# Regrouping an attention loop on TensorE: score and value matmuls in longer runs, four tiles of exponentials, and two smaller buffers paid for it

## The chip, the cores and the metric

The kernel runs on one core of one Trainium2 chip. The metric is the device time of one launch in microseconds (us). The kernel before takes 4168.1 us, the median of three runs that lie between 4166.77 and 4168.17 us. The profiled execution spans 4169.3 us.

## The reference

One vision-transformer layer on 16 images. For each image:

```
h    = patches(x) @ W.T + b                    # 1024 tokens of 768 numbers -> 256
q, k, v = split(layernorm(h) @ w_qkv)          # 8 heads of 32
k    = sum_f a_f*sin(f*k) + b_f*cos(f*k)       # f = 1..256, elementwise ("kan")
h   += softmax(q @ k.T / sqrt(32)) @ v @ w_out + b_out
y    = layernorm(h)
h   += shared_mlp(y) + sum over the top 2 of 4 experts of weight * expert(y)
```

All of it is float32. The Fourier transform of the keys is done by angle addition: a slow wave (two tiles `w`, sines of multiples of 16) is mixed on TensorE with coefficients into `kan`, multiplied on VectorE by a fast wave (`f`), and summed over rows by a matmul with a 0/1 matrix (`red`).

## The kernel before

**Tiling of the work.** An image has 32 groups of keys (`NG`), worked on in rounds of 4 (`GS`): 8 rounds an image, 128 rounds in all. A pair of heads and half of the queries make one attention step (`att`), and each round also does one attention step, two rounds behind the keys it needs. An attention step has eight tiles of keys (`kc` 0 to 7). For each there is a `score` (matmul into PSUM tile `sT`, L1085, followed by `exponential` on ScalarE into an SBUF tile `es`, L1100) and a `weigh` (matmuls of `es` with the values into the PSUM tile `av`, L1117). The value matmul's weights hold 32 columns of values and 32 of ones, so row sums come along.

**Order of TensorE.** Everything is emitted by a planner written in Python (`run`, L398) that holds a modelled clock for each engine and a queue of steps for each. TensorE's own queue is fixed: in a round, the wave mixing (`mix`, L978) and first half of the sums (`add_up`, L1007), then the attention step. The fixed order of the attention step comes from the loop in L1234: with s for a score, r for the second half of the sums, w for a weigh, it is `ssss r ww ss ww ss wwww`. Everything else of the layer (tokens, norms, keys, queries, values, projections, gates and networks) lies in four chains of pieces that the planner inserts between fixed steps, when the next fixed step would have to wait by its model, or when a chain has work due (`PACES`, L57: for each chain a pace per us of fixed work and a limit of what can fall due).

**Matmuls in tiles.** Three kinds of fixed step use a part of the array at a time, so that several matmuls run side by side (`TILINGS`, L59): `kan` in 64x32, `av` in 128x64, `red` in 128x32. Scores and almost all pieces of the chains use the whole array. The planner charges 0.18 us in its model (`SWITCH`) for going from one form to another.

**Buffers the change touches.** `es` tiles come from a ring of three (`esp`, L92); an exponential therefore waits for the weigh of three tiles before (L1103). PSUM has two large tiles (`big`), shared by scores and `kan`, so a score waits for the exponential two scores back. Chunks of x (128 tokens, 384 KB) come from a ring of `XBUFS` = 3 (L45); after a chunk is used the load of the chunk three later is queued (L495). In `keys` (L513) VectorE divides keys by a turn: the integer number of turns goes to tile `n` (L536, a buffer of its own), and after the reduction the angle goes to two tiles `u` and `ui` of a ring of two each (`rup`, tags "u" and "r"), which DMAs write to DRAM (L552). `split` (L558) uses the same two tags for the high and low parts of queries and keys, which DMAs also carry off.

Of the kernel before, what the change touches and what calls it, by code (L numbers as in the profile page):

```python
# [18 lines left out]
P = 128  # L19
# [4 lines left out]
NT = N // P  # L24
# [16 lines left out]
INT = mybir.dt.int32  # L41
FPR = mybir.dt.float32r
BAND0 = 88
XT = 128
XBUFS = 3  # L45
SUM_MAX = 1e20
PACK0 = 18
NW = 8
# [5 lines left out]


LAG, LANDS, TABLE, PER_COLUMN, SWITCH, IDLE = 0.06, 2.0, 1.28, 1.0 / 600, 0.18, 0.3
PACES = ((0.155, 2), (0.44, 2), (0, 0), (0.178, 2.6))  # L57

TILINGS = {"mix": (64, 32), "av": (128, 64), "red": (128, 32)}  # L59

@with_exitstack
def plain_path(ctx: ExitStack, tc: tile.TileContext, a: dict, out: bass.AP, verdict: bass.AP):
# [14 lines left out]
    def pool(name, bufs, space=None):  # L77
        kw = {} if space is None else {"space": space}
        return ctx.enter_context(tc.tile_pool(name=name, bufs=bufs, **kw))

    const = pool("const", 1)
    xp = pool("xp", XBUFS)
    hp = pool("hp", 6)
# [3 lines left out]
    kup = pool("kup", 1)  # L87
    rup = pool("rup", 2)
    wp = pool("wp", NW)
    fp = pool("fp", GS)  # L90
    srcp = pool("srcp", 1)
    esp = pool("esp", 3)  # L92
    q4p = pool("q4p", 2)
    ffp = pool("ffp", 1)
    ff2 = pool("ff2", 2)
# [140 lines left out]
    def retile(tiling):  # L236

        same = now["tiling"] == tiling
        now["tiling"] = tiling
        return 0.0 if same else SWITCH  # L240

    def together(at, queue):

        (cost, _, key, _), *rest = queues[PE][queue][:2]
        tiling = TILINGS.get(key[0])
        if tiling is None or now["tiling"] == tiling or not rest or rest[0][2][0] != key[0]:
            return at
        then = begin(PE, rest[0][1])
        return at + 2 * IDLE if then is None else max(at, then - cost)
# [6 lines left out]
    def side_tile(name):  # L256

        i = chains[now["chain"]]["bank"] = banks(now["chain"])[0][1]
        return side.tile([P, 512], FP, tag=f"side{i}", name=name)
# [91 lines left out]
    def lay(engine, queue):  # L351
        cost, deps, key, action = queues[engine][queue].pop(0)
        at = begin(engine, deps)
        if engine == PE:
            cost += retile(TILINGS.get(key[0]))
        clock[engine] = at + cost
        done[key] = clock[engine]
        if engine == PE:
            for ch, (pace, most) in zip(chains, PACES):
                ch["due"] = min(ch["due"] + pace * cost, most)  # L360
# [37 lines left out]
    def run():  # L398

        while True:  # L400
            soonest = others(clock[PE])
            fixed = min(heads(PE), default=None)
            then = fixed and together(fixed[0], fixed[2])
            follows = fixed and TILINGS.get(queues[PE][fixed[2]][0][2][0]) == now["tiling"] != None
            pieces = [
# [69 lines left out]
    def tokens(b, half):  # L475
# [5 lines left out]
        for t in range(4):  # L481
# [12 lines left out]
            del chunks[b, j]  # L494
            load_x(b, j + XBUFS)  # L495
            yield DVE, 0.41
# [16 lines left out]
    def keys(b, rows, blks=(0, 1)):  # L513

        st = images[b]
        if b >= 2:
            yield "load", NG * (b - 1) - 1, 1
            yield "source", (NG * (b - 1)) // 8 - 1
        if "ud" not in st:
            st["ud"] = udp.tile([E, 2, 2, N], INT, tag="ud", name="ud")  # L520
        for blk in blks:
            yield "hnT", b, blk
            yield GO
            ps = side_tile("k")
            for c in range(2):
                matmul(
                    out=ps,
                    lhsT=wk[:, c, ts(rows, P)],
                    rhs=hnT[:, c, ts(blk, 512)],
                    start=(c == 0),  # L530
                    stop=(c == 1),
                )
            held = chains[now["chain"]]["bank"]
            yield DVE, 1.4
            chains[now["chain"]]["bank"] = held
            n = kup.tile([P, 512], INT, tag="n", name="turns")  # L536
            nc.vector.tensor_scalar(n, ps, INV_2PI, None, ALU.mult)
            nc.vector.scalar_tensor_tensor(ps, n, -TWO_PI_A, ps, ALU.mult, ALU.add)
            yield DVE, 1.4
            chains[now["chain"]]["bank"] = held  # L540
            for part in (TWO_PI_B, TWO_PI_C):
                nc.vector.scalar_tensor_tensor(ps, n, -part, ps, ALU.mult, ALU.add)
            yield DVE, 1.4
            u = rup.tile([P, 512], FP, tag="u", name="u")
            ui = rup.tile([P, 512], INT, tag="r", name="ui")
            uh = u.bitcast(INT)
            nc.vector.tensor_scalar(u, ps, INV_2PI_REST * 2.0**31, None, ALU.mult)
            nc.vector.scalar_tensor_tensor(ui, ps, INV_2PI * 2.0**31, u, ALU.mult, ALU.add)
            yield POOL, 1.02
            nc.gpsimd.tensor_tensor(uh, ui, quarter.to_broadcast([P, 512]), ALU.add)  # L550
            for i, x in enumerate((uh, ui)):
                nc.sync.dma_start(  # L552
                    out=st["ud"][ts(rows, P), i, :, ts(blk, 512)],
                    in_=x.unsqueeze(1).to_broadcast([P, 2, 512]),
                )
            done["rows", b, rows, blk] = sent(2.7, 1.2)
# [156 lines left out]
    def gates(b, half, late=False):  # L713
# [20 lines left out]
        now["stream"] += 2 * P  # L734
        now["piece"] = TILINGS["red"]
        yield ACT, 0.25
# [17 lines left out]
    def networks(b, half, late=False):  # L754
# [29 lines left out]
        def second_of_experts(u, e1):  # L784
            yield GO
            ps = side_tile("e2p")
            now["piece"] = TILINGS["av"]
            now["stream"] -= 512
# [291 lines left out]
    def score(att, kc):  # L1080
        def action():
            q4 = bands_of_queries[att]
            ps = scores[kc] = big.tile([P, 1024], FP, tag="big", name="sT")
            for s in range(2):
                nc.tensor.matmul(  # L1085
                    out=ps[:, ts(s, 512)],
                    lhsT=k4[:, 2 * s + kc // 4, ts(kc % 4, P)],
                    rhs=q4[:, s, :],
                    start=True,
                    stop=True,  # L1090
                )

        deps = [("stacked", att // 2), ("q4", att)] + big_deps(("exp", att, kc))
        put(PE, "fixed", 0.47, deps, ("score", att, kc), action)

    def exponential(att, kc):
        def action():
            now["table"] = AF.Exp
            es = exps[kc] = esp.tile([P, 1024], FP, tag="es", name="es")
            nc.scalar.activation(es, scores.pop(kc), AF.Exp, scale=SCALE)  # L1100

        deps = [("score", att, kc)]
        old = att * NT + kc - 3  # L1103
        if old >= 0:
            deps.append(("av", *divmod(old, NT)))
        put(ACT, "fixed", 0.99, deps, ("exp", att, kc), action)

    def weigh(att, kc):

        p = att // 2  # L1110

        def action():
            if kc == 0:
                acc[0] = avp.tile([P, 512], FP, tag="av", name="av")
            es = exps.pop(kc)
            for s in range(2):
                nc.tensor.matmul(  # L1117
                    out=acc[0][ts(s, 64), :],
                    lhsT=v[:, kc, p % NPAIR, ds(HD * s, 64)],
                    rhs=es[:, ts(s, 512)],  # L1120
                    start=(kc == 0),
                    stop=(kc == NT - 1),
                )

        deps = [("exp", att, kc)]
        if kc == 0:
            b, i = divmod(p, NPAIR)
            deps.append(("all values" if i == NPAIR - 1 else "values", b))
            if att > 0:
                deps.append(("norm", att - 1))  # L1130
        put(PE, "fixed", 0.86, deps, ("av", att, kc), action)
# [49 lines left out]
    queues[SP]["source"] = []  # L1181
    for j in range(XBUFS):
        load_x(0, j)
# [32 lines left out]
    for rd in range(B * RI + 2):  # L1216
        groups = range(GS * rd, min(GS * rd + GS, total))
        att = rd - 2
        attends = 0 <= att < ATT
        for g in groups[::2]:  # L1220
            first = g == groups[0]
            for i, j in ((0, 0), (0, 1), (1, 0), (1, 1), (0, 2), (1, 2)):
                sine(g + i, j, TABLE if first and i == j == 0 else 0.0)
            mix(g)
            mix(g + 1)
        if groups:
            add_up(groups[0] // 2)

        def table():
            now["table"] = AF.Exp  # L1230
            nc.scalar.activation(spare[:, 1:2], spare[:, 0:1], AF.Exp)  # L1231

        put(ACT, "fixed", TABLE + 0.2, [], ("table", rd), table)
        for n in range(0, NT + 2, 2):  # L1234
            if attends and n < NT:
                for kc in (n, n + 1):
                    score(att, kc)
                    exponential(att, kc)
            if n == 2 and groups:
                add_up(groups[0] // 2 + 1)  # L1240
            if attends and n > 0:
                for kc in (n - 2, n - 1):
                    weigh(att, kc)
    with tc.manual_schedule():
        run()

# [746 lines left out]
```

## Time and profile before

| what | value |
|---|---|
| median time | 4168.1 us |
| TensorE busy | 4027.4 us, 97% of the span |
| ScalarE, GpSimd, VectorE busy | 3286.3, 3195.8, 2830.2 us |
| DMA engines busy | 79% on the main queue, 219 GB/s |
| `av` matmuls | 965.1 us busy |
| `sT` matmuls | 691.7 us busy |
| `kan` matmuls | 623.9 us busy |
| exponentials | 1024 of 1022 ns |

Busy time counts each engine's own work; the matmuls' ends are modelled, so a busy TensorE may still be emptying its array or loading weights. The chain of waits is read backwards from the last instruction and names, for every stretch, the engine that held the program up there.

### The profile page before, as it was taken

To read this page: it belongs to the slowest core of one execution; us is meant where nothing else is said; L and a number is where in the kernel's file an instruction comes from. 1 tells how busy PE (TensorE), PEld (TensorE's weight loads), DVE (VectorE), ACT (ScalarE), POOL (GpSimd) and SP (SyncE) were. 2 spreads that over 40 slices of the span, in tenths; PEclk is the share of its full clock that TensorE was granted. 3 is DMA by queue.
4 is the path that set the end of the run, shared out by engine and by line. 5 is a ranking of instruction groups with operands and counts; after the bars stand their busy time and mean duration, and the time that the engine had idled before them with its cause. 6 is when DMAs were issued, how large, how long until landed. Compare 5 with 4: busy or idle time off the path is not lost.

```text
span 4169.3 us, 67564 instructions
## 1 busy us (share of the span) xinstructions
PE 4027.4 (97%) x22753; PEld 1766.4 (42%) x22753; DVE 2830.2 (68%) x4172; ACT 3286.3 (79%) x3939; POOL 3195.8 (77%) x2323
## 2 busy tenths in 40 slices
PE   6889999999999999999999999999999999999998
PEld 4324344443434445344444444444444444443334
DVE  4667767677676776767767677776767767677652
ACT  2688888788787888878788888788788788888873
POOL 3988877778787887878787787888778787787850
PEclk9999999999999999999999999999999999999999
DMA  7988878888787887978878878887887978878740
GB/s 223 263 241 222 243 200 223 238 218 247 207 232 219 239 235 210 244 211 224 247 209 238 221 225 225 228 241 209 234 228 219 251 211 239 219 211 226 197 138 16
DMA packets 587478, 914.27 MB, mean 219 GB/s; under 512 B 58828, under 2 KB 177524, under 8 KB 587124
## 3 DMA queue, kind: packets, MB, share of 16 engines
q1 hardware_dynamic: 580880, 906.98, 78.7%
q8 instruction: 184, 3.01, 0.3%
q10 hardware_dynamic: 6244, 2.88, 0.3%
q14 instruction: 170, 1.39, 0.1%
HBM read 758.64 MB, written 150.99 MB: 218 GB/s over the span
## 4 chain that ended last, share of the span: by engine, by line
PE 74%; ACT 10%; DVE 6%; DMA 5%; issue 3%; SPq 2%; POOL 1%; ACTq 0%; DVEq 0%; POOLq 0%
PE av L1117 18%; PE sT L1085 11%; PE kan L987 9%; PE tok L263 6%; PE e3p L263 5%; PE red L1020 5%; PE e1p L263 5%; ACT w L963 4%; DMA w<-ud 3%; PE s1p L263 3%; PE q L263 2%; PE v L263 2%; PE proj L263 2%; DVE f L1001 2%; PE k L263 2%
## 5 line engine op out<-in xcount | busy, mean ns | idle before, releaser
L953 POOL TENSOR_TENSOR w<-w,lane 128x1024 int32<-128x1024 int32 x1024 | 1926.1, 1896 | 444.4 <-DMA w<-ud 298.6
L1100 ACT ACTIVATE es<-sT 128x1024 f32<-128x1024 f32 x1024 | 1033.0, 1022 | 550.0 <-PE av L1117 339.8
L953 POOL TENSOR_TENSOR f<-f,lane 128x1024 int32<-128x1024 int32 x512 | 971.0, 1896 | 251.2 <-DVE f L938 157.5
L963 ACT ACTIVATE w<-w 128x1024 f32<-128x1024 int32 x1024 | 1021.1, 1048 | 42.1 <-POOL w L953 39.1
L1117 PE MATMUL av<-es,v 128*64 128x512 f32 x4096 | 965.1, 602 | 1.0 <-DVE rc L1162 1.0
L1143 DVE RECIPROCAL rc<-av 128x256 f32<-128x256 f32 x256 | 434.0, 1730 | 702.6 <-PE av L1117 702.6
L1085 PE MATMUL sT<-q,k 128*128 128x512 f32 x2048 | 691.7, 449 | 42.0 <-DVE f L1001 20.2
L1001 DVE TENSOR_TENSOR f<-kan,f 128x1024 f32<-128x1024 f32 x512 | 608.5, 1218 | 159.8 <-ACT f L963 123.7
L938 DVE STREAM_SHUFFLE f<-src 128x1024 int32<-128x1024 int32 x512 | 673.0, 1353 | 0.7
L987 PE MATMUL kan<-w,coef 64*32 64x512 f32 x8192 | 623.9, 600 | 39.5 <-ACT w L963 35.6
L1085 PEld LDWEIGHTS sT<-q,k 128*128 128x128 f32 x2048 | 346.0, 189 | 440.5 <-issue 219.0
L963 ACT ACTIVATE f<-f 128x1024 f32<-128x1024 int32 x512 | 516.1, 1048 | 2.6 <-POOL f L953 2.6
L1117 PEld LDWEIGHTS av<-es,v 128*64 128x64 f32 x4096 | 258.5, 136 | 563.2 <-issue 498.2
L263 PE MATMUL tok<-wt,x 128*128 128x256 f32 x1536 | 362.3, 387 | 16.9 <-DMA w1s<-in_sW 13.6
L263 PEld LDWEIGHTS tok<-wt,x 128*128 128x128 f32 x1536 | 288.7, 192 | 110.8 <-issue 34.7
L987 PEld LDWEIGHTS kan<-w,coef 64*32 64x32 f32 x8192 | 127.9, 105 | 375.2 <-ACT w L963 222.5
L1020 PE MATMUL red<-f,pack 128*32 128x512 f32 x2048 | 273.6, 604 | 1.5 <-DVE f L1001 1.3
L263 PE MATMUL e1p<-hT,w1e 128*128 128x512 f32 x480 | 233.2, 608 | 0.4 <-ACT e L799 0.4
L462 ACT ACTIVATE hn<-h,less,rstd 128x256 f32<-128x256 f32 x256 | 143.8, 591 | 51.6 <-POOL less L454 51.2
L963 ACT ACT_TABLE_LOAD x128 | 164.2, 1283 | 22.4 <-DMA w<-ud 20.2
L1150 DVE TENSOR_TENSOR aT<-av,rc 32x512 f32<-32x512 f32 x256 | 176.1, 688 | 6.4
L1231 ACT ACT_TABLE_LOAD x128 | 164.2, 1283 | 2.2
(125 smaller groups left out, 3746.7 us busy)
## 6 DMA issues: line engine op xcount, KB each, us to landing
w<-ud SPq DMA_DIRECT2D x2048, 256.0 KB
q<-qd SPq DMA_DIRECT2D x512, 128.0 KB
k<-kd SPq DMA_DIRECT2D x128, 512.0 KB
x<-in_xT SPq DMA_DIRECT2D x128, 384.0 KB
ud<-u SPq DMA_DIRECT2D x64, 512.0 KB
ud<-ui SPq DMA_DIRECT2D x64, 512.0 KB
src<-ud SPq DMA_DIRECT2D x512, 64.0 KB
qd<-qhi SPq DMA_DIRECT2D x64, 256.0 KB
```

The costliest lines, as they stand in the source:

```text
L263: nc.tensor.matmul(out=out, lhsT=lhsT, rhs=rhs, start=start, stop=stop)
L938: nc.vector.stream_shuffle(w, sources[g // 8].rearrange("p r n -> p (r n)"), [4 * (g % 8) + i // 8 for i in range(32)],)
L953: nc.gpsimd.tensor_tensor(w, w, f.to_broadcast([P, N]), ALU.mult)
L963: nc.scalar.activation(x, w, AF.Sin, scale=TURN * 2.0**-32)
L987: nc.tensor.matmul(out=ps[ds(64 * j + 32 * blk, 32), ts(r, 512)], lhsT=coef[ts(r, 64)].rearrange("p e f j -> p (e f j)"), rhs=w[ts(r, 64), ...
L1001: nc.vector.tensor_mul(w, kan.pop(g), w)
L1020: nc.tensor.matmul(out=rows_of_pair[p][ts(2 * i + r, 32), :], lhsT=pack[:, ds(PACK0 - 16 * (k % 2) - 2 * (k // 2), 32)], rhs=prod[:, ts(r, ...
L1085: nc.tensor.matmul(out=ps[:, ts(s, 512)], lhsT=k4[:, 2 * s + kc // 4, ts(kc % 4, P)], rhs=q4[:, s, :], start=True, stop=True,)
L1100: nc.scalar.activation(es, scores.pop(kc), AF.Exp, scale=SCALE)
L1117: nc.tensor.matmul(out=acc[0][ts(s, 64), :], lhsT=v[:, kc, p % NPAIR, ds(HD * s, 64)], rhs=es[:, ts(s, 512)], start=(kc == 0), stop=(kc == ...
L1143: nc.vector.reciprocal(rc[0][:, part], acc[0][:, part])
L1150: nc.vector.tensor_mul(aT[ds(64 * (i % 2) + HD * s, HD), i // 2, ts(qb, 512)], acc[0][ds(96 * s, HD), :], rc[0][ds(HD + HD * s, HD), :],)
```

## The change

The attention step's order is written as a string, and its two runs of weighs are made longer: `ssss r ss www ss wwwww`. That needs one more tile of exponentials, since six scores stand ahead of the first weigh. A tile of exponentials is 4 KB a partition; the memory comes from a chunk of x (3 KB) and the tile of whole turns (2 KB), which now takes its place in the ring tagged "u". The chains' paces are set anew.

```diff
-XBUFS = 3
+XBUFS = 2
...
-PACES = ((0.155, 2), (0.44, 2), (0, 0), (0.178, 2.6))
+PACES = ((0.18, 1.5), (0.42, 2.5), (0, 0), (0.16, 2))
...
+ES = 4
+ATTENTION = "ssssrsswwwsswwwww"
...
-    esp = pool("esp", 3)
+    esp = pool("esp", ES)
...
-            n = kup.tile([P, 512], INT, tag="n", name="turns")
+            n = rup.tile([P, 512], INT, tag="u", name="turns")
...
-        old = att * NT + kc - 3
+        old = att * NT + kc - ES
...
-        for n in range(0, NT + 2, 2):
-            if attends and n < NT:
-                for kc in (n, n + 1):
-                    score(att, kc)
-                    exponential(att, kc)
-            if n == 2 and groups:
+        scored, weighed = iter(range(NT)), iter(range(NT))
+        for kind in ATTENTION:
+            if kind == "r" and groups:
                 add_up(groups[0] // 2 + 1)
-            if attends and n > 0:
-                for kc in (n - 2, n - 1):
-                    weigh(att, kc)
+            elif kind == "s" and attends:
+                kc = next(scored)
+                score(att, kc)
+                exponential(att, kc)
+            elif kind == "w" and attends:
+                weigh(att, next(weighed))
```

## The prediction

> **What bounds the kernel now.** I read the shares of busy time first, then the busy time of one image's stretch from the middle, then TensorE's waits, and last the chain of waits inside one attention step.
>
> ```profile
> PE 4027.4 (97%) x22753; PEld 1766.4 (42%) x22753; DVE 2830.2 (68%) x4172; ACT 3286.3 (79%) x3939; POOL 3195.8 (77%) x2323
> ```
> ```profile
> 2000.00:2260.00 260.00, 257.07 (x1477) 117.53 (x1478) 184.72 (x273) 211.16 (x253) 201.08 (x146) 1.00 0.80 224
> ```
> The second line (us, then busy time of PE, PEld, DVE, ACT, POOL, then clock, DMA share and GB/s) says that in the middle TensorE is busy 257 of 260 us, at full clock, and that no other engine passes 211. So TensorE's stream of instructions is the bound, and only what shortens it, or removes a wait in it, counts.
>
> ```profile
> PE kan L987 <- ACT w L963: 35.6, 41, 3.7
> PE sT L1085 <- DVE f L1001: 20.2, 46, 1.0
> PE sT L1085 <- ACT es L1100: 15.4, 38, 1.0
> PE tok L263 <- DMA w1s<-in_sW: 13.6, 1, 13.6
> ```
> These are the longest of TensorE's waits (us in total, times, longest). They are small, so waits alone can't bring much. But TensorE is not doing useful columns all of its busy time. The chain of waits in one attention step (start, us, what):
>
> ```profile
> 2010.06 0.93 PE sT L1085 x4
> ...
> 2013.64 0.99 PE red L1020 x8
> 2014.64 1.87 PE av L1117 x8
> 2016.50 1.12 PE sT L1085 x4
> 2017.63 1.87 PE av L1117 x8
> 2019.49 1.13 PE sT L1085 x4
> 2020.62 3.58 PE av L1117 x16
> ...
> 2028.71 1.88 PE kan L987 x32
> ...
> 2033.46 1.36 PE kan L987 x16
> ...
> 2037.42 1.02 PE kan L987 x16
> ```
> Eight more av matmuls in one run cost 3.58 - 1.87 = 1.71 us, so a run of eight carries 1.87 - 1.71 = 0.16 us that don't depend on its length. Four sT matmuls cost 0.93 us between other whole-array matmuls and 1.12 to 1.13 between runs of av: 0.20 us for standing between two runs of another form. For kan, 1.88 - 1.02 = 0.86 for sixteen, so 1.02 - 0.86 = 0.16 a run. These fixed parts are counted as busy.
>
> **What the Trainium skill says.** "TensorEngine Tiling (Array Packing)", Tiling Modes, Key Properties: changing the tiling mode, as against the tile, drains TensorE. It gives no price; this trace agrees, with 0.16 to 0.20 us a run. "TensorE: Matmul & The Clock Gate", Part 1, on the architecture: ScalarE's and VectorE's queues are strict FIFO, so a VectorE instruction that waits holds all behind it. The trace agrees as far as it shows: the cast to qhi waited 6.8 us for the DMA that carries ui off, and VectorE did nothing meanwhile.
>
> **The change part by part.**
>
> *Fewer changes of form (gain).* Before, a step's fixed order has three runs of av (ww, ww, wwww), afterwards two (www, wwwww); whole-array runs stay three, and the sums one. That is one run less in 128 steps, unless pieces of the chains cut runs. I counted the runs of equal form in the order in which both built programs give TensorE its matmuls: 1863 before and 1707 after. Of 128x64 (av and the experts' second layer) 433 to 311, of the whole array 762 to 746, of kan's form 349 to 332, of red's 286 to 285. All other matmuls are the same in number. So 122 x 0.16 + 16 x 0.20 + 17 x 0.16 = 19.5 + 3.2 + 2.7 = 25.4 us less, all on the path, since it comes out of TensorE's own stream.
>
> *Waits of scores on exponentials.* Each score reuses the PSUM tile of two scores before. Let the step start at 0: scores take 0.46, an exponential 1.03. Exponentials end at about 1.55, 2.6, 3.6 and 4.65. Score 3 can start at 2.6, both before and after; then red to 4.05, the return to the whole array 0.2, score 4 to 4.7, and score 5 needs the end of the fourth exponential at 4.65: it needs no wait. After www (2.6 + 0.16), scores 6 and 7 need exponentials 4 and 5, which start when the first and second weigh free their tiles and take 1.03 each; the second ends about with the start of score 7. So 0; where no piece fills in, 0.3 us in some 40 steps, 12 us, is the upper bound.
>
> *ScalarE free sooner (gain).* With three tiles the last exponential waits for weigh 4; three weighs of 0.86 are left on TensorE, so ScalarE turns to the next sines 3 x 0.86 - 1.03 = 1.55 us before TensorE's end of the step. With four tiles it waits for weigh 3 and is free 4 x 0.86 - 1.03 = 2.4 us before: 0.86 us sooner. This is worth something only where kan waits for a sine: 35.6 us in 41 waits, 0.87 in the mean. Bounds 0 and 35; I take 10, since sines also queue behind other ScalarE work that moves with the paces.
>
> *Two chunks of x.* The load of chunk j+2 now starts when chunk j is used. From the end of a chunk's matmuls to landing, the trace has about 3 us at the start (the packets of 512 bytes are x's alone) and 3 to 8 us later. In the order after, the tightest places in the middle leave 7 us of TensorE work, so I take no wait there. At the start, tokens stand back to back, 2.6 us a chunk, and landing takes 3.1 to 3.8: about 0.5 us every second chunk and 0.8 at the first. For the eight chunks of image 0: 2 us, straight into the span; bounds 1 and 4.
>
> *Whole turns in the ring of angles.* n, u and the low parts now alternate between two buffers. A u follows the u before by one n, so it waits until that one's DMA has landed. A u is reusable after 0.68 (u) + 0.69 (ui) + 1.04 (GpSimd's quarter turn) + 4.4 (from issue to landing, where qhi waited for ui's) = about 7 us. In the order after, VectorE has only 4.1 to 4.9 us of work between two u at seven places: three at the start and four in the middle. In four more places n follows a klo by 2.1 us, and klo's DMA must land: 0.69 + about 4.4 - 2.1 = 3 us. At the start about 3 us each; the first waves need only the first two u, which stand 12 us apart, so I charge 3 (bounds 0 and 7). In the middle 8 x 3 = 24 us of VectorE waiting; what is queued behind are shuffles and products f, and through the products (which free kan's PSUM) TensorE. VectorE is idle 75 of 260 us, so most is absorbed: 6 (bounds 0 and 24).
>
> *Paces.* They move pieces only; what they do to the runs is in the count. 0.
>
> Sum: -25.4 + 0 - 10 + 2 + 3 + 6 = -24.4 us: 4168.1 - 24.4 = 4143.7, say 4144.
>
> **The rivals.** (A) *More than the runs:* ScalarE's head start removes kan's waits (35.6 us) instead of a third of them, and the new waits are absorbed: -25 - 35 + 5 = -55, 4113. For it: the head start equals the mean wait. Against: the longest wait is 3.7 us, so the sum has few long ones that 0.86 doesn't remove. (B) *A new wait takes the gain:* VectorE's wait for the angles' DMAs reaches TensorE in full (24 + 7), x costs 4, kan gains 10: -25 + 31 + 4 - 10 = 0; with half of it, 4160. For it: VectorE is strict FIFO, and DMA is busy 80%, so landing can be slow. Against: the idle share. (C) *Slower:* B in full (0), and steps without a piece wait on exponentials (12), and DMAs land in 8 us, the slowest of x's landings, instead of 4.4: 3.6 us more at 15 places, 54 us, of which I let a quarter reach TensorE (13): 4168 + 25 = 4193. For it: in the first 320 us DMA is the busiest part, where VectorE already waited 6.8 us. Against: sizes and number of the DMAs are as before.
>
> **How the numbers follow.** Forecast 0.63, A 0.14, B 0.15, C 0.08. The range is 4116 to 4166: below, two thirds of A's way; above, most of B; C is left out. Faster by over 0.2% (below 4159.8) are the forecast, A and a part of B: 0.82; within 0.2% 0.10; slower 0.08.
>
> **What would show it.** Right: runs of av of 12 and 20 matmuls in the chain, each 0.16 over 1.71 for eight; TensorE's busy time down by about 25 us; kan's wait for ScalarE below 30; a wait of u or turns on the DMA of ud or kd of some 3 us at some ten places on VectorE, and a few tok waiting for x in the first 40 us. Wrong: if TensorE's idle time grows by more than 20 us, with f or the ring at the head of its waits, or if ScalarE's waits for av don't shrink from 339.8 us.

## The result and the profile after

The changed kernel takes 4194.47 us (median of four runs, 4192.8 to 4204.7) against 4168.04 us: ratio 1.0069, with a 95% interval of 1.0052 to 1.0087. It is slower by 26 us, where 4144 us had been forecast. The profiled executions span 4169.3 and 4190.8 us, 21.5 us apart; the accounts below are of these.

The line of busy times of the changed kernel:

```profile
PE 4008.7 (96%) x22753; PEld 1777.1 (42%) x22753; DVE 2832.2 (68%) x4172; ACT 3273.8 (78%) x3939; POOL 3194.1 (76%) x2323
```

TensorE is busy 4027.4 - 4008.7 = 18.7 us less. But its idle time went from 4169.3 - 4027.4 = 141.9 to 4190.8 - 4008.7 = 182.1 us, 40 us more. The busy time of the same stretch in the middle (us, then PE, PEld, DVE, ACT, POOL, clock, DMA share, GB/s):

```profile
2000.00:2260.00 260.00, 254.78 (x1487) 112.55 (x1485) 185.16 (x268) 214.25 (x257) 207.16 (x149) 1.00 0.83 227
```

TensorE is still the bound, at full clock. Its idle time in the stretch has grown from 2.9 to 5.2 us. The changed kernel's waits of TensorE (us in total, times, longest):

```profile
PE kan L989 <- ACT w L965: 42.3, 43, 4.8
PE sT L1087 <- ACT es L1102: 33.6, 62, 4.0
PE sT L1087 <- DVE f L1003: 17.0, 43, 1.2
...
PE tok L265 <- DMA x<-in_xT: 5.9, 5, 1.8
PE v L265 <- DVE qlo L567: 4.6, 5, 1.2
```

Scores now wait 33.6 us for exponentials (15.4 before), `kan` waits 42.3 us for sines (35.6 before; the forecast had it shrink), and tokens wait for x. Pieces of the chains wait longer too: by the groups of the profile, TensorE's idle time went from 0.4 to 7.3 us ahead of `e1p`, from 0.8 to 6.2 ahead of `gate` and from 0.5 to 5.5 ahead of `v`, and fell from 6.4 to 2.5 ahead of `wb`. One step of attention, from the chain of waits of the changed kernel (start, us, what):

```profile
2014.36 1.91 ACT es L1102 x2
2016.27 0.04 issue
2016.32 0.74 PE sT L1087 x2
2017.05 0.99 PE red L1022 x8
2018.05 1.92 PE k L265 x4
2019.96 0.94 PE sT L1087 x4
2020.90 2.73 PE av L1119 x12
2023.62 1.12 PE sT L1087 x4
```

The chain comes to this step through ScalarE: score 3, the first line of TensorE, starts only when the second of two exponentials has ended. The run of twelve `av` matmuls takes 2.73 us, just what the forecast's price gives (0.16 + 12 x 1.71 / 8 = 2.73). A piece (`k`) now stands between the sums and the fifth score, a place where the kernel before needed none, since two weighs stood there.

**Where the 21.5 us are.** I cut TensorE's stream of each trace into its runs of equal form. From the start of one run to the start of the next there are three parts: the columns of its matmuls at the interval that they keep inside long runs, the fixed price of one run (0.16 for `kan`, 0.15 for 128x64, 0.10 for `red`, 0.20 for the whole array), and a rest, which is mostly waiting. From the first matmul to the last:

```
us                               before   after
columns                          3530.9  3530.9
fixed price of the runs           302.1   277.5   (-24.6; forecast -25.4)
rest: waiting                     314.2   360.2   (+46.0; forecast about +1)
```

The second line is the count of runs times the price of one; that the price holds is shown by the long runs, which take what it gives. The third is what is left, and it grows by about as much as TensorE's idle time in the profile (40 us). To place it, I took for each score the time since the start of the matmul ahead of it, less the time that the quickest tenth of such pairs of matmuls takes in these traces. Ahead of the eight scores of a step this sums to 62 us before and 90 us after; scores 1, 3 and 5 grow by 8 to 9 us each (the fifth from 0.3 to 9.5), the others by less than 2. Another 8.5 us are new in the first eight rounds, where x is loaded (some 2 of them ahead of scores), and about 11 us are spread over the rest of the stream. So the gain of the runs came as forecast, and new waits took it and more.

### The profile page after: what moved, and what is told of

It is laid out like the page before. It is cut to its first block, busy times and chain, and to the rows that moved or that the text cites. A ratio compares the mean times of both kernels' runs of the same rounds, so it can differ in the third digit from the quotient of the medians.

```text
span 4190.8 us, 67571 instructions
## 1 busy us (share of the span) xinstructions
PE 4008.7 (96%) x22753; PEld 1777.1 (42%) x22753; DVE 2832.2 (68%) x4172; ACT 3273.8 (78%) x3939; POOL 3194.1 (76%) x2323
## 4 chain that ended last, share of the span: by engine, by line
PE 62%; ACT 14%; DMA 11%; DVE 6%; issue 3%; SPq 2%; POOL 1%; ACTq 0%; DVEq 0%; POOLq 0%
PE av L1119 15%; PE sT L1087 10%; PE kan L989 7%; ACT w L965 6%; DMA w<-ud 5%; PE tok L265 5%; PE e3p L265 5%; PE e1p L265 4%; PE red L1022 4%; ACT f L965 3%; PE proj L265 2%; PE s1p L265 2%; DVE f L1003 2%; PE k L265 2%; PE v L265 2%
## 5 line engine op out<-in xcount | busy, mean ns | idle before, releaser
L1102 ACT ACTIVATE es<-sT 128x1024 f32<-128x1024 f32 x1024 | 1015.6, 1022 | 540.6 <-PE av L1119 294.0
L1119 PE MATMUL av<-es,v 128*64 128x512 f32 x4096 | 935.4, 598 | 0.1
L1087 PE MATMUL sT<-q,k 128*128 128x512 f32 x2048 | 707.6, 452 | 57.9 <-ACT es L1102 33.6
L989 PE MATMUL kan<-w,coef 64*32 64x512 f32 x8192 | 606.6, 601 | 44.9 <-ACT w L965 42.3
L1087 PEld LDWEIGHTS sT<-q,k 128*128 128x128 f32 x2048 | 337.2, 189 | 512.1 <-ACT es L1102 251.4
L1119 PEld LDWEIGHTS av<-es,v 128*64 128x64 f32 x4096 | 271.3, 136 | 532.7 <-issue 508.8
L552 POOL TENSOR_TENSOR u<-ui,quarter 128x512 int32<-128x512 int32 x64 | 66.4, 1038 | 132.4 <-DVE ui L550 127.5
```

What stands on the lines that cost most here:

```text
L989: nc.tensor.matmul(out=ps[ds(64 * j + 32 * blk, 32), ts(r, 512)], lhsT=coef[ts(r, 64)].rearrange("p e f j -> p (e f j)"), rhs=w[ts(r, 64), ...
L1087: nc.tensor.matmul(out=ps[:, ts(s, 512)], lhsT=k4[:, 2 * s + kc // 4, ts(kc % 4, P)], rhs=q4[:, s, :], start=True, stop=True,)
L1119: nc.tensor.matmul(out=acc[0][ts(s, 64), :], lhsT=v[:, kc, p % NPAIR, ds(HD * s, 64)], rhs=es[:, ts(s, 512)], start=(kc == 0), stop=(kc == ...
```

## The experiments

All ratios are to the kernel before on the same chip, with 95% intervals. For room, kernels with four tiles of exponentials and three chunks of x use the keys' weights for the queries and the values' weights for the output projection (same shapes, other numbers).

**The parts of the change, one at a time.** First the two buffers, each alone:

```diff
-XBUFS = 3
+XBUFS = 2
```

> The kernel before with only two chunks of x in place of three; TensorE's order is unchanged. Theory W, its smaller part: 2 to 8 us at the start, where the tokens stand back to back: 4170 to 4176. Theories O and P: within 6 us of 4168.

Measured: 4179.33 us, 1.0027 [1.0016, 1.0039], or +11 us by the ratio (8 between the medians of that chip). The run's waits of TensorE have a new line, `tok` on the load of x:

```profile
PE tok L263 <- DMA w1s<-in_sW: 13.4, 1, 13.4
PE lnT L267 <- ACT hn L462: 8.4, 9, 3.5
PE tok L263 <- DMA x<-in_xT: 6.5, 5, 1.8
```

From the first matmul to the end of the eighth round this kernel takes 309.9 us instead of 299.4. Later it loses nothing; its profiled execution even gets 6 us back, which the median doesn't show. So the place was right and the size was not: 8 to 11 us, not 2.

```diff
-            n = kup.tile([P, 512], INT, tag="n", name="turns")
+            n = rup.tile([P, 512], INT, tag="u", name="turns")
```

> The kernel before with only the whole turns put into the ring of angles; TensorE's order is unchanged. Theory W: VectorE waits for the DMAs of angles, and TensorE with it, +15 to +35 us: 4183 to 4203. Theories O and P: within 6 us of 4168.

Measured: 4170.09 us, 0.9999 [0.9992, 1.0006]. The turns in the ring cost nothing. In the changed kernel too, VectorE waits less than 1 us in all for a DMA ahead of `u` or the turns, where the forecast had 24 us in the middle alone.

The new paces alone, and the new order alone with the old paces (three chunks of x, a tile of its own for the turns):

```diff
-PACES = ((0.155, 2), (0.44, 2), (0, 0), (0.178, 2.6))
+PACES = ((0.18, 1.5), (0.42, 2.5), (0, 0), (0.16, 2))
```

> The kernel before with only the new paces. 1793 runs of equal form on TensorE against 1863, priced at about 12 us. Theory F (the order with six scores in front opens waits that the pieces of the chains must fill, and the paces only move pieces): within 15 us of before, 4156 to 4172. Theory P (these paces suit the kernel in themselves): 4150 or below, as the new order lost 40 us without them.

```diff
+ES = 4
+ATTENTION = "ssssrsswwwsswwwww"
-    esp = pool("esp", 3)
+    esp = pool("esp", ES)
```

> The kernel before with only the new order of the attention step and four tiles of exponentials (paces, three chunks of x and the own tile of turns as before). To make room, queries are computed with the keys' weights and the output projection with the values' weights: same work, other numbers. TensorE's runs of equal form: 1664 against 1863 before, priced at 0.15 to 0.20 us each about 32 us. Theory W (the two smaller buffers brought the new waits): this kernel keeps the gain, about 4168 - 32 = 4136, with no more idle time of TensorE than before. Theory O (the new order itself makes TensorE wait for exponentials): idle time of TensorE grows by 25 us or more and the time is 4160 or over.

Measured: paces alone 4187.32 us, 1.0038 [1.0024, 1.0053], or +16; order alone 4228.59 us, 1.0148 [1.0131, 1.0165], or +62, with only 1664 runs of equal form and 401 us of waiting. The expectation for the paces alone, within 15 us and not above 4172, failed. Their waits show that a new placing of the pieces makes scores wait for exponentials in the old order too (15.4 us before):

```profile
PE sT L1085 <- ACT es L1100: 28.0, 33, 3.5
```

Both together:

> The kernel after, its order on TensorE instruction for instruction, but with three chunks of x and the own tile of turns; queries and output projection with other weights to make room, as in the run with the order alone. 1707 runs of equal form. Theory W: the new waits go with the buffers, about 4194 - 46 = 4148. Theory P (the paces put pieces where they wait): still near 4190, while the run with the order alone is 25 us or more faster. Theory O: both near 4190.

Measured: 4187.98 us, 1.0052 [1.0036, 1.0069], or +22; fixed prices 277.5 us, waiting 352.9 us, and 30 us more ahead of scores than before, as in the changed kernel (28). So the buffers aren't the cause of the main loss: with the old ones it is there. The paces don't add up with the order: +16 alone, -40 on top of it. A price of their own can't be given.

**The ring of the angles' tiles.** The planner knows nothing of when the DMAs let go of these tiles, and VectorE waited for them in the changed kernel (VectorE's waits):

```profile
DVE khi L566 <- DMA ud<-ui: 19.9, 5, 7.1
DVE qhi L566 <- DMA qd<-qhi: 13.7, 7, 2.9
DVE qhi L566 <- DMA ud<-ui: 10.5, 2, 7.3
```

That is 44 us, where the same three have 16.8 us before. To see what of it reaches TensorE, the ring was made three deep (for room, w1s and w3e are aliased as well):

```diff
-    rup = pool("rup", 2)
+    rup = pool("rup", 3)
```

> The new order with four tiles and new paces (three chunks of x, own tile of turns), and the ring of angles and of high and low parts three deep in place of two. To make room, queries, output projection, the first shared layer and the experts' last layer are computed with other weights. TensorE's order is unchanged. Theory R (part of the new waits is TensorE behind VectorE, which waits until an angles' or a part's DMA has landed): the waits of q and v, about 11 us above before's, go: 10 to 15 us under the run with two tiles. Theory S (waits before scores are all of it): within 5 us of it.

Measured: 4173.7 us, 1.0002 [0.9993, 1.0011], 14 us (medians) to 21 us (ratios) below the same kernel with two; waiting falls by 10 us, to 343.1. So a part of the loss goes through this ring, by the split into high and low parts and not by the turns. But the waits ahead of scores stay (28 us above before), and the gain of the runs still doesn't come out. Then the old order with four tiles and the new paces, with two and three tiles in the ring:

```diff
-ATTENTION = "ssssrsswwwsswwwww"
+ATTENTION = "ssssrwwsswwsswwww"
```

> The old order of the attention step (ssss r ww ss ww ss wwww) with four tiles of exponentials and the new paces; three chunks of x, own tile of turns; queries and output projection computed with other weights to make room. 1815 runs of equal form, priced at about 9 us under before. Theory F (the order makes the waits): 4150 to 4168, and TensorE's unpriced waits no more than before's. If the fourth tile or the new paces make them: 4180 or more, as with the new order.

> The old order with four tiles and the new paces, which took 4296 us, with the ring of angles and parts three deep (the first shared layer and the experts' last layer also with other weights to make room). TensorE's order is unchanged. Theory R: the 79 us by which q and v wait longer than before's go for the most part: 4210 to 4240. If the order of pieces itself makes them: 4280 or more.

Measured: 4295.92 us, 1.0298 [1.0281, 1.0316], and 4241.64 us, 1.0158 [1.0141, 1.0175]. In the first, TensorE's waits show how a late DMA reaches it, through VectorE's queue:

```profile
PE q L265 <- DVE qlo L567: 42.6, 8, 7.2
PE sT L1087 <- ACT es L1102: 32.7, 56, 4.5
PE kan L989 <- ACT w L965: 30.8, 43, 3.7
PE v L265 <- DVE qlo L567: 15.2, 7, 4.3
```

VectorE's waits in the same kernel:

```profile
DVE qhi L566 <- DMA ud<-ui: 42.6, 6, 8.5
DVE qhi L566 <- DMA qd<-qhi: 40.8, 7, 7.3
```

A projection `q` waits for its PSUM bank, which `qlo` must empty, and `qlo` stands behind a `qhi` that waits for a DMA. In the old order, with the pieces placed anew around a fourth tile, the kernel is 124 us slower than before and some 108 slower than with the new paces alone; 54 of these go through the ring. What the tile does with all else in place was not measured in the old order. Scores wait 32.7 us for exponentials here, as long as in the changed kernel: the new order is not the only thing that makes such waits.

**Which engine makes the scores wait?** Half of each exponential is left out (both heads' values are weighed with those of the first), with the old order and with the new one:

```diff
-            nc.scalar.activation(es, scores.pop(kc), AF.Exp, scale=SCALE)
+            nc.scalar.activation(es[:, 0:512], scores.pop(kc)[:, 0:512], AF.Exp, scale=SCALE)
```

> The kernel before with each exponential over half of its columns only (the first head's; its exponentials are also weighed with the second head's values), which takes about 0.4 us off each of 1024. TensorE's order is unchanged. It is the partner of the next run. All theories: somewhat faster, 4130 to 4165.

> The new order with four tiles and new paces (three chunks of x, own tile of turns, queries and output projection with other weights), with the same halved exponentials. Compared with the halved exponentials in the old order. Theory S (in the six scores in front TensorE waits for exponentials): those waits go, and the fewer runs show: 15 to 25 us faster than the partner. Theory F in the wide sense (pieces are short in other places too, at the first two scores and in kan): still slower or within 8 us of the partner.

Measured: 4132.83 us, 0.9908 [0.9891, 0.9924], and 4133.18 us, 0.9909 [0.9893, 0.9926]. Both gain, and the new order's loss of 22 us shrinks to nothing; ahead of score 5, 0.3 us are left. But the expected lead of 15 to 25 us over the old order doesn't appear either: the fixed prices are 24.6 us lower, and the waits still 24 us higher than in the old order (299 against 275 us). Halving the exponentials takes away the loss, not all that stands against the gain. Now the sines instead: of one sine in each pair only half the columns are computed, and used twice.

```diff
-            nc.scalar.activation(x, w, AF.Sin, scale=TURN * 2.0**-32)
+            half = slice(0, 512 if j == 1 else N)
+            nc.scalar.activation(x[:, half], w[:, half], AF.Sin, scale=TURN * 2.0**-32)
```

> The kernel before with every second sine of the slow waves over half of its columns (those columns are mixed twice, the other half is left out), which takes 0.43 us off each of 512 sines, 1.7 us of ScalarE a round between the attention steps. TensorE's order is unchanged. It is the partner of the next run. Theory A (ScalarE, full between the steps, sets the pace there): 4110 or below. Theory T (TensorE alone does): 4150 or more.

> The new order with four tiles and new paces (three chunks of x, own tile of turns, queries and output projection with other weights), with the same shortened sines. Theory A: with ScalarE relieved the 24.6 us of fewer changes of form stay, so 12 to 30 us faster than its partner with the old order. If pieces and waits on DMAs alone eat the gain: no faster than its partner, or slower by up to 17 us as with whole sines.

Measured: 4133.28 us, 0.9912 [0.9895, 0.9928], and 4149.45 us, 0.9951 [0.9934, 0.9967]. The loss of the new order is still 16 us, so work of ScalarE between the attention steps matters little to it: of the two expectations, the one in which relief there frees the gain fails. The old order with short sines, at 4133 us, lies between its two (4110 or below, 4150 or more). The two cuts aren't equal: the sines lose 218 us of ScalarE's time, the exponentials 437, so a part of the difference between 16 us and nothing may be due to size. Less work for ScalarE in another way, the copies out of `lnT` on VectorE, with the old kernel and the changed one:

```diff
-            nc.scalar.copy(dst[:, c, :], ps)
+            nc.vector.tensor_copy(dst[:, c, :], ps)
```

> The kernel before, all of its work done, with the copies of the transposed norms (128 of 0.58 us) on VectorE in place of ScalarE. 1842 runs of equal form. Theory A: ScalarE's stretch between the steps shortens by some 0.4 us a round, 20 to 50 us faster than before, 4120 to 4150. Theory T: 4160 or more.

> The kernel after, all of its work done, with the copies of the transposed norms on VectorE. 1712 runs of equal form. Theory A: 20 to 50 us faster than the kernel after, 4145 to 4175, and closer to or ahead of its partner with the old order. Theory T: within 15 us of 4194.

Measured: 4326.12 us, 1.0373 [1.0355, 1.039], and 4324.91 us, 1.0374 [1.0357, 1.0392]. The gains of 20 to 50 us that one expectation had didn't come, and a time near that of the changed kernel, which the other had for the second run, neither. This tells nothing of the dispute: the planner put the pieces elsewhere, and both stand 155 us above the kernel before.

**Other orders with fewer runs.**

```diff
-ATTENTION = "ssssrsswwwsswwwww"
+ATTENTION = "sssssrwwwssswwwww"
```

> The attention step as sssss r www sss wwwww with four tiles and new paces; three chunks of x, own tile of turns; queries and output projection with other weights. The sums go straight over to a run of av, so the whole array comes in two runs a step: 1537 runs of equal form against 1707, priced at 29 us under the new order and 54 under before's. Theory F (what leaves the runs comes back as waits, because pieces to fill with are limited): 4160 or more. If runs count as priced and waits stay: 4188 - 29 = 4159 or below.

```diff
-ATTENTION = "ssssrsswwwsswwwww"
+ATTENTION = "ssssrwwwsssswwwww"
```

> The attention step as ssss r www ssss wwwww, otherwise as the run before: 1577 runs of equal form. Four scores in front as in the old order, but the last of the second four wait for exponentials that start only as the first weighs end. Theory S: scores 4 and 5 wait less than in the new order (by 9 us at score 5), scores 6 and 7 more; no faster than the five in front. If waits stay as in the new order: 4188 - 26 = 4162.

Measured: 4232.68 us, 1.0138 [1.0121, 1.0155], and 4202.39 us, 1.0066 [1.0049, 1.0083]. Against the kernel before, they have 1537 and 1577 runs, fixed prices of 245.0 and 251.8 us, and waits of 433.9 and 397.4 us. In the second, scores wait for exponentials 131 times, 56.2 us; as expected scores 4 and 5 hardly wait and scores 6 and 7 wait longer, but it is 30 us faster than the first, not slower. In both, the waits grow by more than the runs give.

**The order, or the planner's new places?** Up to here, every kernel whose pieces were placed anew had waits of over 342 us where no work was left out, and the others 313 to 318; so it could have been the placing. The last two kernels therefore keep each piece where the kernel before has it, and put the new order into those slots (29 pieces that would cut a run of weighs stand ahead of it). The first has the old buffers, the second those of the change and all work.

```diff
-        run()
+        replay()
```

> The new attention order with four tiles of exponentials, put into the slots of the kernel before: every other piece of work stands where the kernel before has it, not where the planner would put it anew; 29 pieces that would fall inside a run of weighted values are moved ahead of that run. Three chunks of x and a tile of its own for the turns, as before; for room, the projection of queries reads the weights of the keys and the output projection those of the values (same shapes, other numbers). 1722 runs of equal form on TensorE, 305 of 128x64 (before 1863 and 433): by the prices of the forecast (433-305) x 0.152 + 12 x 0.20 = 22 us less. Theory P (placing the pieces anew made the waits): the unpriced waits stay near the 314 us of before, so 4168 - 22 = 4146 us (4138 to 4158). Theory S (six scores in front of the weighted values make the waits by themselves): the waits grow as in the changed order with the old buffers (353 us and more), so 4175 us or more.

> As the run with the new order at the old places, but with the buffers of the changed kernel: two chunks of x, the turns in the ring of angles, and all weights, so that nothing is left out. Theory P: some 11 us above the other run, the measured price of two chunks, so 4157 us (4148 to 4166), and faster than both kernels of this study. Theory S: 4185 us or more.

Measured: 4179.65 us, 1.0022 [1.0015, 1.0029], and 4192.06 us, 1.0049 [1.0035, 1.0062]. So the waits need no new placing: with all pieces in place the fixed prices go down by 21.9 us, the waits go up by 29.9, and the kernel is slower by 9 us. Between the two lie 12 us, the price of two chunks again, and the second takes almost what the changed kernel takes (4194.47). The first run's waits of TensorE:

```profile
PE sT L1166 <- ACT es L1181: 44.7, 80, 1.9
PE kan L1068 <- ACT w L1044: 30.0, 34, 3.7
```

By position, score 5 alone now waits 35.9 us (0.3 before). All scores together wait 47 us longer than before, and waits elsewhere are shorter. In 75 of the 116 rounds from the ninth to the 124th, score 5 starts within 0.13 us of the end of exponential 3, in the changed kernel in 53, in the kernel before in 3. This is the mechanism, laid bare in one step, first as the chain of waits of the kernel with the new order in the old places:

```profile
2014.87 0.93 PE sT L1166 x4
2015.80 0.99 PE red L1101 x8
2016.80 1.36 PE sT L1166 x4
2018.16 2.73 PE av L1198 x12
2020.88 1.13 PE sT L1166 x4
2022.02 4.44 PE av L1198 x20
```

Its `av` takes 2.73 + 4.44 = 7.17 us. The same step of the kernel before (its lines from 2013.64 on, in the prediction) takes 1.87 + 1.87 + 3.58 = 7.32: 0.15 us are gained. But scores 4 and 5, now right behind the sums, take 1.36 instead of 1.12: 0.24 us are lost. The timeline of ScalarE in this kernel shows the reason (start, us, what, then the idle time before it and what ended that):

```profile
2015.43 1.94 ACT L1181 ACTIVATE es<-sT 128x1024 f32<-128x1024 f32 x2 [0.70 <-PE sT L1166]
2019.27 1.94 ACT L1181 ACTIVATE es<-sT 128x1024 f32<-128x1024 f32 x2 [1.90 <-PE av L1198]
```

Exponentials 2 and 3 run from 2015.43 to 2017.37. Exponential 2 had to wait for score 2, and exponential 3 runs behind it. Score 5 takes the PSUM tile of score 3. The second matmul of score 4 starts at 2017.07 and takes 0.23, so TensorE would reach score 5 at 2017.30; it starts it at 2017.43. In the kernel before, two weighs (1.87 us) stood between the sums and score 4, and covered all this.

The larger part comes where ScalarE has a piece of the chains ahead of exponential 3. In one and the same step (ScalarE's timeline), first the kernel before, then the new order in the old places:

```profile
1170.86 1.93 ACT L1100 ACTIVATE es<-sT 128x1024 f32<-128x1024 f32 x2
1172.89 1.58 ACT L462 ACTIVATE hn<-h,less,rstd 128x256 f32<-128x256 f32 x3
1174.78 1.03 ACT L1100 ACTIVATE es<-sT 128x1024 f32<-128x1024 f32 x1 [0.30 <-PE av L1117]
```
```profile
1172.51 1.93 ACT L1181 ACTIVATE es<-sT 128x1024 f32<-128x1024 f32 x2
1174.48 1.58 ACT L543 ACTIVATE hn<-h,less,rstd 128x256 f32<-128x256 f32 x3
1175.98 1.00 ACT L1181 ACTIVATE es<-sT 128x1024 f32<-128x1024 f32 x1
```

Three normalizations, 1.58 us, stand ahead of exponential 3 in both. Before, ScalarE even had to wait for a weigh afterwards; TensorE was doing `ww` (two weighs) and lost nothing. With the new order score 5 waits for that exponential, 1.2 us in this step. In those 116 rounds, the 47 with such a piece lose 27.2 us ahead of score 5, the 69 without it 7.8; in the kernel before all 116 lose 0.3. In the changed kernel the planner has moved some of these pieces away (26 such rounds, 2.4 us), waits ahead of scores 1 and 3 come in, and the time is 8 us higher than in the old places (medians of 4187.98 against 4179.65 us, both with the old buffers).

The waits of its scores for exponentials in the 116 rounds can be sorted by what ScalarE did between the end of a score and its exponential: 24 us have a piece there (11 before), and 24 us exponentials alone (12 before), 14 of these at score 3 (3 before). So half of the growth is the FIFO of ScalarE with a piece at its head, and half is scores that stand back to back with no cover on TensorE, as in the step shown at the top. How much of this comes from the order, and how much from the placing that goes with the new paces, is not separated in the changed kernel; the kernels with the old places show it for the order alone.

## Why the prediction was wrong, step by step

**What bounds the kernel**: right. TensorE's stream sets the time; its busy time fell, and the time rose by its waits alone.

**Fewer changes of form**: right. The count times the price gives -24.6 us against -25.4, and runs of 12 and 20 carry the same 0.16 us. TensorE's busy time, for which the forecast had about 25 us less, fell by 18.7: that of `av` and `kan` fell by 47 together, but that of the scores rose from 691.7 to 707.6.

**Waits of scores on exponentials**: this is the step that failed. It was put at 0, with 12 us as the upper bound; measured are +28 us ahead of scores in the changed kernel (+18 of it plain idle time for exponentials, 15.4 to 33.6), and +47 with the pieces in their old places. Two things were wrong in its working. It had score 5 reach its tile at 4.70 with the exponential done at 4.65, and took the 0.05 us for safety. That was one step without pieces and without the time from a score's last column to its exponential (0.26 us where ScalarE is free) and from the exponential to the next score (0.05). Where exponential 2 waits for score 2, as in the step at 2015.43, these decide. And it let ScalarE do nothing but exponentials, while with the old places a piece stands ahead of exponential 3 in 47 of 116 rounds. It named steps where no piece fills in as the exposed ones; they are one half of it (24 us with exponentials alone, 12 before), the pieces of ScalarE the other. The weighs between sums and scores were not only a change of form: they were what these waits hid behind. "TensorE: Matmul & The Clock Gate" in the Trainium skill, Part 1, gives ScalarE a strict FIFO queue; the forecast used it for VectorE and forgot ScalarE. The trace agrees: exponential 3 ran only after the three normalizations, 1.58 us, though its score was ready.

**ScalarE free sooner**: the head start is there in part, the gain isn't. ScalarE's wait of exponentials for weighs shrank from 339.8 to 294.0 us, and from the start of the first exponential to the end of the last a step takes 13.60 us instead of 14.01, half of the 0.86 us that were worked out. But `kan` waits 42.3 us for sines, not below 30. With the old places it shrinks (30.0), by half of the 10 us that were forecast.

**Two chunks of x**: right in place, wrong in size. 8 to 11 us alone, 12 us in the last pair and 6.5 between the changed kernel and the one with the old buffers; in each pair of traces the first eight rounds take 10 us longer, against 2 us with a bound of 4. The working took 0.5 us every second chunk from TensorE's side. The visible waits of `tok` on x sum to about 6 us; how the rest comes about in the start isn't shown.

**Turns in the ring**: wrong, 0 instead of 9 us. The waits that were feared are under 1 us. What waits in this ring are the high parts of queries and keys, 44 us of VectorE; a deeper ring is worth 14 to 21 us (2 of them in the first eight rounds, where that kernel also loads two weights less). How much of that the kernel before would gain too wasn't tried.

**Paces**: 0 was no answer. Alone they cost 16 us, under the new order they save 40. "They move pieces only" left out that a moved piece can wait itself (`e1p`, `gate` and `v`, above) and can leave a score without cover.

The sum: -24.6 (runs) + 28 (scores) + 8.5 - 2 (x, without its part ahead of scores) = 10 us of the 21.5 us between the traces; the rest lies among the waits of pieces and of `kan` and was not taken apart. The rival that ended slower had the right side and almost the time (4193), but mostly for other reasons: it counted VectorE's waits on DMAs in full. Its term on exponentials, 12 us, was less than half of what came. The forecast's own sign of failure came true in its first half: idle time grew by 40 us, more than the 20 named. But neither `f` nor the ring stands at the head of the growth, as it had them; the exponentials do (+18 us). Two sums of the forecast are also off: half of B's new wait gives 4153 and not 4160, and the lower end of the range, 4116, lies nine tenths of the way to A and not two thirds.

## What to carry to other kernels

A change of form on TensorE has a price that the trace gives to a few per cent, but the short run that is taken away may also be the cover under which another engine catches up: before lengthening runs, list for each wait in the loop what stands between producer and consumer on TensorE, and what else stands in the producer's queue. A margin of 0.05 us in a hand-made timeline is no margin; the hops between engines alone took 0.31 us here. Where a planner places the rest of the work, replay the old places with only the change under test: it separates the change from the re-planning, which moved the time here by 8 us under one and the same order, and by 40 us between two sets of paces.

## What the runs showed of the hardware

- From the last column of a score to the start of its exponential 0.26 us pass where ScalarE is free (the median of 223 in the changed kernel, nine tenths of them below 0.27), and 0.05 us from an exponential's end to the score that reuses its tile.
- The price of a run of `av` doesn't depend on its length: 12 and 20 matmuls of 128x64 took 2.73 and 4.44 us, and 0.16 + 0.214 for each gives the same.
- Carrying a tile off by DMA held VectorE up to 8.5 us (`qhi` behind `ui`, in the old order with four tiles, DMA engines busy 78%).
